# A fused attention block on one core: weights' sums, one load's place and the order of the tokens' small steps in setup and batches 0 and 1

## The chip, the cores and the metric

The kernel runs on one core of one Trainium2 chip. The metric is the device time of one execution, in microseconds (us); lower is better. Time before: 973.11 us, the median of 3 runs (971.55 to 974.76).

## What is computed

For each of 16 batches there are 100 rows `x` of 640 numbers and a context of 722 rows of 384. The last 4 context rows are "tokens" (`ca`), the other 718 are `enc`. All arithmetic is float32. Cut to what matters:

```
hs     = mha(x @ Wq, enc @ Wk, enc @ Wv)              # 8 heads of 80, 718 keys
ca_q1  = einsum("btc,th->bch", ca, Wq_ca)[:, picked]  # 100 picked columns of the tokens
ca_hs1 = mha(ca_q1, x, x)                             # first token attention
hs2    = mha(ca_hs1 @ Wq, ca @ Wk_ca, ca @ Wv_ca)     # second token attention, 4 keys
out    = (hs + hs2) @ Wout + b_out + x
mha    = softmax(q k^T / sqrt(80)) v, head by head
```

## The kernel before

**Products with fewer multiplications.** The context of a batch, seen as 3 thirds of the rows by 3 chunks of 128 columns, is multiplied with Wk and with Wv, each seen as 3 chunks by 2 halves. A bilinear scheme does this with 15 products in place of 18. Each product takes a form of the context (7 are raw pieces, the others are sums of pieces, made by `enc_sums`, L466 to L485, 13 operations on GpSimd) and a form of the weights (6 raw, others made by `weight_sums`, L487 to L506: 7 "early" ones that fill unused slots and 5 "late" ones, some of which overwrite raw pieces). `V_PLAN` (L93) and `K_PLAN` (L111) give the order of the products, the PSUM bank of each (A to E), and where the bank's content is moved to afterwards. The first move to a place is a copy on ScalarE (L392), a later one an addition on VectorE (L390). `Keys.go(n)` and `Values.go(n)` issue the next n products with their moves. A bank that was opened goes on collecting, so its next product must come after the move of the content before it.

**Batch 0 is different.** Its values (`first_values`, L353) and its keys (`first_keys`, L561) are made plainly from raw pieces, because the sums don't exist yet. Two of its six value blocks (0 and 3) are made only inside batch 0, between the key products of batch 1.

**Setup (L256 to L1082).** Loads go out on SP, in an order that is partly fixed. TensorE makes `first_values`, a matrix `m` for the tokens (L1007), the tokens' products `y_ps` (L721), and turns the packed Wk by transposes into `w_ps` (L1030). Five copies of `w_ps` into `wk_sb` and `wk4` go alternately to ScalarE and VectorE (L1033). On VectorE stand also 15 copies that rearrange Wq (L1041, L1048). Then come the first keys, `va_ps`, and the queries of batches 0 and 1.

**The loop over batches (L1090).** One batch, in the order of TensorE: scores `s_ps` (L598, three groups, each moved to SBUF by ScalarE), the first token attention's `z_ps` (L783), the next batch's token products `y_ps` (L721), the transposes of the batch before, then the products of this batch's values and the next batch's keys in turn, `last_keys` (L568), the output projection of the batch before, on odd batches the next queries (L519), and last `a_ps` (L1267), the probabilities times the values.

- `Maximum` (L634) makes the maximum over the keys, for each head and query, in five steps (`top.go`), mostly on VectorE. `subtract(i)` and `exponential(i)` turn the scores into probabilities on VectorE and ScalarE; `larger(i)` keeps the running maximum.
- The tokens' small steps belong to the class `Second` (L703): `scores1` (7 operations of GpSimd, L756 and L763), `softmax1` (VectorE, 8 steps of a `Maximum` and a subtraction), `exponentials1` (ScalarE), `softmax2` (L778), `scores2` (3 operations of VectorE and an exponential of ScalarE), `softmax3` (3 of VectorE) and `values2` (7 of GpSimd, L845 and L852). `load` brings the token values `vb` by GpSimd's DMA queue (L802; one buffer).
- `keys(m)` (L691, 5 operations of GpSimd) prepares a batch's token keys. `loads()` (L1096) asks for the batch after next: `ca`, the context (`load_enc`, L213: three transfers, two buffers) and `mb` (`load_m`, L682, two buffers). `load_rest` (L223) asks for the two pieces of the context that have a buffer of their own, `rest`, of which there is one. An mb load waits until `keys` has read the buffer's content.

**What sets the order.** From L1089 on, TensorE, VectorE, ScalarE and GpSimd issue in the order of the Python text (`manual_schedule`). Before that line, and on SP throughout, a planner chooses the order from its own estimate of when things are ready. `tc.issue_after(ins)` keeps what its block holds behind `ins` on that engine, and `wait_for(a, b)` (L623) makes `a` wait for `b`.

Of the kernel before, what the change touches and what calls it, by code (L numbers as in the profile page):

```python
# [14 lines left out]
B, S, H = 16, 100, 640  # L15
# [7 lines left out]
KT = SK // 3 + 1  # L23
# [101 lines left out]
def kernel(  # L125
# [63 lines left out]
    def hsT_tile(name):  # L189
        return main.tile([P, HC, P], F32, tag="hsT", name=name, bufs=2)  # L190
# [19 lines left out]
    def rest_tile(name):  # L210
        return main.tile([P, len(A_REST), KT], F32, tag="rest", name=name)
# [9 lines left out]
        return enc  # L221

    def load_rest(b, enc):  # L223
        rest = rest_tile(f"rest_{b}")
        for (u, c), i in A_REST.items():
            nc.sync.dma_start(
                out=rest[:, i], in_=enct[b][:, c, u * (KT - 1) : u * (KT - 1) + KT]
            )
        return enc[0], rest
# [257 lines left out]
    def weight_sums(engine, w, late):  # L487

        at = lambda f: w[:, W_AT[f]]
        raw = lambda c, g: w[:, 2 * (c - 1) + g - 1]  # L490
        for out, left, right in (
            (at(5), raw(2, 2), raw(1, 2)),
            (at(14), raw(2, 1), raw(2, 2)),
            (at(7), raw(3, 2), at(5)),
            (at(3), raw(1, 1), at(7)),
            (at(13), raw(3, 1), at(7)),
        ) if late else (
            (at(0), raw(1, 2), raw(1, 1)),
            (at(1), raw(2, 1), raw(3, 1)),
            (at(2), raw(1, 1), raw(2, 2)),  # L500
            (at(6), raw(2, 1), raw(1, 1)),
            (at(10), raw(3, 1), raw(2, 2)),
            (at(11), raw(2, 2), raw(3, 2)),
            (at(12), raw(3, 2), raw(3, 1)),
        ):
            engine.tensor_tensor(out, left, right, ALU.subtract)  # L506
# [54 lines left out]
    def first_keys(enc):  # L561
        for n in range(HC - 1):
            banks = [psum(f"kT_ps_0_{n}_{k}") for k in range(2)]
            weights = [wk_sb[:, 2 * c + n % 2, n // 2] for c in range(CC)]
            chunk_keys(n, banks, weights, enc)
        last_keys(0, enc)
# [460 lines left out]
    for c in range(HC):  # L1027
        w_ps = psum(f"w_ps_{c}")
        for cc in range(CC):
            nc.tensor.transpose(  # L1030
                w_ps[:, cc * P : (cc + 1) * P], wkt_sb[:, c, cc * P : (cc + 1) * P], ident
            )
        (dve if c % 2 else act)(  # L1033
            wk_sb[:, c % 2 : 6 : 2, c // 2] if c < HC - 1 else wk4,
            w_ps[:, : CC * P].rearrange("p (a n) -> p a n", a=CC),
        )

    with tc.issue_after(summed.ins):
        for c in range(HC):
            for u in range(2):  # L1040
                nc.vector.tensor_copy(  # L1041
                    wq_sb[:, c, 2 * u * P : 2 * (u + 1) * P].rearrange(
                        "p (a r k) -> p a r k", a=2, r=RG
                    ),
                    wq_in[c].rearrange("p (r k) -> p r k", r=RG)[:, :, u * D : u * D + 64]
                    .rearrange("p r (a k) -> p a r k", a=2),
                )
            nc.vector.tensor_copy(  # L1048
                wq_sb[:, c, 4 * P :].rearrange("p (h k) -> p h k", h=NH),
                wq_in[c].rearrange("p (h k) -> p h k", h=NH)[:, :, 64:],  # L1050
            )
    first_keys(enc)

    va = wide("va")[:, : H // 2]
    va_ps = psum("va_ps")
# [34 lines left out]
    for b in range(B):  # L1090
# [38 lines left out]
        if b == 0:  # L1129
            now.load()  # L1130
            now.softmax1()
            for late in (False, True):
                weight_sums(nc.vector, wk_sb, late)
            enc_sums(enc)
            weight_sums(nc.gpsimd, wv_sb, False)
        st.append(scores(b, 0, tiles))
        if b == 0:
            now.exponentials1()
# [14 lines left out]
            kk = Keys(b + 1, enc)  # L1153

        if b == 0:
            now.scores2()
            now.softmax3()
            second.scores1()
            top.go(3)
            kk.go(3)  # L1160
            top.go(1)
            first_values(3, e_in, (act, act), (0,), bank)
            kk.go(2)
            top.go()
            first_values(3, e_in, (act, act), (1,), bank)
            kk.go(3)
            first_values(0, e_in, (act, act), (0,), bank)
            kk.go(2)
            subtract(0)
            exponential(0)  # L1170
            first_values(0, e_in, (act, act), (1,), bank)
            kk.go(2)
            subtract(1)
            kk.go(3)
            exponential(1)
            second_next, enc_next, m_next = loads()
            last_keys(b + 1, enc)
            subtract(2)
            exponential(2)
            now.values2()  # L1180
            second.load()
            second.softmax1(4)
        elif b + 1 < B:
            last.transpose()
            vv = Values(b, e_in)

            def both(n):
                vv.go(n)
                kk.go(n)

            second.scores1(seen)
            last.load()
            top.go(3)
            both(3)
            now.scores2()
            top.go(1)
            both(2)
            top.go()
            both(2)
            both(1)  # L1200
            now.softmax3()
            now.values2()
            vv.go(2)
            kk.go(1)
            subtract(0)
            exponential(0)
            both(2)
            vv.go(1)
            kk.go(2)
            both(1)  # L1210
            both(1)
            second.load()
            second_next, enc_next, m_next = loads()
            subtract(1)
            exponential(1)
            last_keys(b + 1, enc)
            subtract(2)
            exponential(2)
            second.softmax1()
            last.project()  # L1220
        else:
            room = enc_tile("spare").rearrange("p f k -> p (f k)")
            spare.extend(room[:, i * H : (i + 1) * H] for i in range(2))
            last.transpose()
            vv = Values(b, e_in)
            last.load()
            mine.load()
            top.go(3)
            vv.go(3)
            now.scores2()  # L1230
            top.go(1)
            vv.go(2)
            top.go()
            vv.go(3)
            now.softmax3()
            now.values2()
            vv.go(2)
            subtract(0)
            exponential(0)
            vv.go(5)  # L1240
            for i in (1, 2):
                subtract(i)
                exponential(i)
            last.project()
        if b + 2 < B:
            enc_next = load_rest(b + 2, enc_next)
            keys(m_next)
            enc_sums(enc_next)
# [97 lines left out]
```

## Time and profile before

| What | Value |
|---|---|
| median of the runs, with lowest and highest | 973.11 us (971.55 to 974.76) |
| the profiled execution's own time | 972.35 us |
| its span, from the first to the last instruction | 970.6 us |
| TensorE clock granted, mean | 0.993 of full speed |
| TensorE matmul busy | 942.7 us |
| VectorE, GpSimd, ScalarE busy | 674.4, 627.4, 359.5 us |
| moved by DMA | 62.48 MB in 45255 packets |

The profile is of one execution. Its engines are PE (TensorE matmuls), PEld (TensorE weight loads), DVE (VectorE), ACT (ScalarE), POOL (GpSimd) and SP (SyncE, which only issues transfers here). A "q" behind an engine's name is its sequencer, as in SPq for a transfer that SP issues. In a line of a timeline stand the start and the length in us, the engine, the line of the code, the operation, what it writes and reads, and in brackets how long the engine had been idle and who ended that. Times count from the start of the span. An adjacent run of equal instructions is shown as one line with its count. The lines that matter are shown in the prediction.

### The profile page before, as it was taken

The page shows a single profiled execution, that of the slowest core. Times are in us where ns is not written, and L with a number is a line of the kernel's source. Part 1 is how long each engine was busy: PE and PEld are TensorE (multiplying, and loading weights), DVE is VectorE, ACT ScalarE, POOL GpSimd, SP SyncE. Part 2 cuts the span into 40 slices and gives each one's busy share as a digit, 9 for nine tenths or more (in the row PEclk, how much of TensorE's full clock was granted, in tenths as well). Part 3 has the DMA queues.
Part 4 walks back from the last instruction along what each step waited for, and adds up shares of the span by engine and source line. Part 5 has one row for each costly group of instructions (what it writes and reads, how often), then busy time and mean ns, then how long its engine had stood idle before and what let it go on. Part 6 is the DMA issues. An engine that isn't in the chain of part 4 may idle for free.

```text
span 970.6 us, 25628 instructions
## 1 busy us (share of the span) xinstructions
PE 942.7 (97%) x11215; PEld 803.1 (83%) x11215; DVE 674.4 (69%) x1083; ACT 359.5 (37%) x596; POOL 627.4 (65%) x572
## 2 busy tenths in 40 slices
PE   8898879999999999999999999999999999999998
PEld 5797868988788888978889887897879888897866
DVE  1358769586856868587874868668784877838783
ACT  1134424433334343342534334343432534324341
POOL 4269877594963758487673958638694576737522
PEclk9999999999999999999999999999999999999999
DMA  7840213113030211213031030301103030300101
GB/s 244 286 146 23 66 34 92 32 25 103 8 119 24 71 58 28 73 29 120 9 105 38 8 121 8 119 24 49 52 29 99 8 102 17 85 27 1 58 1 35
DMA packets 45255, 62.48 MB, mean 64 GB/s; under 512 B 13336, under 2 KB 37208, under 8 KB 43544
## 3 DMA queue, kind: packets, MB, share of 16 engines
q1 hardware_dynamic: 41608, 42.97, 14.9%
q0 software_dynamic: 2512, 16.72, 5.5%
q8 instruction: 88, 1.44, 0.6%
q10 hardware_dynamic: 1024, 1.15, 0.4%
q14 instruction: 23, 0.19, 0.1%
HBM read 55.26 MB, written 5.57 MB: 63 GB/s over the span
## 4 chain that ended last, share of the span: by engine, by line
PE 81%; POOL 7%; DMA 4%; DVE 3%; SPq 2%; ACT 1%; issue 1%; ACTq 0%; DVEq 0%; POOLq 0%
PE a_ps L1267 11%; PE s_ps L598 10%; PE v_psA L419 9%; PE v_psB L419 8%; PE k_psA L450 7%; PE o_ps L926 7%; PE q_ps L519 6%; PE k_psB L450 6%; PE kT_ps L543 5%; PE v_psC L419 3%; PE k_psC L450 2%; POOL enc L485 2%; PE v_psE L419 1%; POOL e L756 1%; PE y_ps L721 1%; PE v_psD L419 1%
## 5 line engine op out<-in xcount | busy, mean ns | idle before, releaser
L756 POOL TENSOR_TENSOR e<-ca,g 100x800 f32<-100x800 f32 x64 | 99.4, 1563 | 147.5 <-DVE most L1124 131.9
L845 POOL TENSOR_TENSOR hs<-vb,p 100x640 f32<-100x640 f32 x64 | 105.6, 1660 | 43.9 <-DVE p L831 41.3
L1267 PEld LDWEIGHTS a_ps<-vs,st 120*64 120x64 f32 (+3 forms) x3072 | 112.4, 127 | 11.1 <-ACT st L1120 5.9
L1267 PE MATMUL a_ps<-vs,st 120*64 120x81 f32 (+3 forms) x3072 | 115.6, 237 | 5.4 <-ACT st L1120 5.4
L419 PE MATMUL v_psA<-wv_sb,enc 128*120 128x320 f32 x360 | 112.1, 434 | 1.5 <-DVE vs L390 1.5
L1112 DVE TENSOR_TENSOR st<-st,over 120x1600 f32<-120x1600 f32 x48 | 106.2, 2236 | 0.0
L485 POOL TENSOR_TENSOR enc<-enc 128x240 f32<-128x240 f32 x135 | 98.6, 745 | 7.1
L485 POOL TENSOR_TENSOR enc<-enc,rest 128x240 f32<-128x240 f32 x45 | 40.0, 888 | 95.6 <-DMA rest<-in_enct 82.0
L598 PE MATMUL s_ps<-qp,kT 32*120 32x100 f32 x3072 | 97.4, 263 | 0.0
L598 PEld LDWEIGHTS s_ps<-qp,kT 32*120 32x120 f32 x3072 | 94.7, 179 | 1.6 <-issue 0.2
L763 POOL TENSOR_TENSOR e<-e,e 100x800 f32<-100x800 f32 x48 | 93.3, 1943 | 3.8
L450 PE MATMUL k_psA<-enc,wk_sb 128*128 128x240 f32 x360 | 88.8, 370 | 6.2 <-POOL enc L485 3.4
L419 PE MATMUL v_psB<-wv_sb,enc 128*120 128x320 f32 x300 | 93.1, 433 | 0.0
L615 ACT COPY st<-s_ps 120x800 f32<-120x800 f32 x64 | 49.7, 829 | 114.8 <-PE s_ps L598 114.8
L450 PEld LDWEIGHTS k_psA<-enc,wk_sb 128*128 128x128 f32 x360 | 68.6, 191 | 24.0 <-POOL enc L485 3.9
L419 PEld LDWEIGHTS v_psA<-wv_sb,enc 128*120 128x120 f32 x360 | 64.5, 183 | 24.7 <-DVE vs L390 2.7
L1124 DVE TENSOR_TENSOR most<-most,st 120x800 f32<-120x800 f32 x64 | 65.5, 1023 | 23.0 <-ACT st L609 21.9
L1120 ACT ACTIVATE st<-st 120x1600 f32<-120x1600 f32 x48 | 74.0, 1542 | 17.9 <-DVE st L1112 17.9
L852 POOL TENSOR_TENSOR hs<-hs,hs 100x640 f32<-100x640 f32 x48 | 77.1, 1607 | 3.8
L450 PE MATMUL k_psB<-enc,wk_sb 128*128 128x240 f32 x300 | 73.9, 369 | 0.0
L1278 DVE RECIPROCAL rs<-a_ps 100x4 f32<-100x4 f32 x32 | 5.8, 182 | 97.7 <-PE a_ps L1267 97.6
L419 PEld LDWEIGHTS v_psB<-wv_sb,enc 128*120 128x120 f32 x300 | 54.8, 183 | 22.3 <-DVE vs L390 0.5
(138 smaller groups left out, 1791.5 us busy)
## 6 DMA issues: line engine op xcount, KB each, us to landing
vb<-va_d POOLq DMA_DIRECT2D x16, 1000.0 KB, 5.9
enc<-in_enct SPq DMA_DIRECT2D x30, 240.0 KB, 3.8
enc<-in_enct SPq DMA_DIRECT2D x15, 360.0 KB, 3.7
xT<-in_xt SPq DMA_DIRECT2D x8, 500.0 KB, 3.5
rest<-in_enct SPq DMA_DIRECT2D x31, 120.0 KB, 3.6
xn<-in_x SPq DMA_DIRECT2D x11, 320.0 KB
out<-xn SPq DMA_DIRECT2D x11, 320.0 KB, 2.5
ca<-in_cas SPq DMA_DIRECT2D x16, 156.2 KB
```

Of the source, the lines that this page charges most:

```text
L419: nc.tensor.matmul(at[0][j][:KN, : H // 2], a_form(self.enc, f)[:, j * KN : (j + 1) * KN], wv_sb[:, W_AT[f]], start=first, stop=last, skip ...
L450: nc.tensor.matmul(at[:, i * KT : (i + 1) * KT], wk_sb[:, W_AT[f], i], a_form(self.enc, f), start=(first and i == 0), stop=last, skip_grou ...
L485: nc.gpsimd.tensor_tensor(out, left, right, op)
L598: nc.tensor.matmul(s_ps[r][:n, 256 * a + lo : 256 * a + hi], kT[rows, c, u, j * KN : (j + 1) * KN], rhs, start=(a == 0 and c == 0), stop=( ...
L756: first = nc.gpsimd.tensor_tensor(to, self.ca[:, t, :].unsqueeze(1).to_broadcast([S, NH, S]), g[:, :, t].unsqueeze(2).to_broadcast([S, NH, ...
L763: nc.gpsimd.tensor_tensor(e, e, to, ALU.add)
L845: first = nc.gpsimd.tensor_tensor(to, vb[:S, t, :].rearrange("p (h d) -> p h d", h=NH), p2[:, :, t].unsqueeze(2).to_broadcast([S, NH, D]), ...
L852: nc.gpsimd.tensor_tensor(sums, sums, to, ALU.add)
L926: nc.tensor.matmul(o_ps[:n, k, : H // 2], hsTs[r][:, c, :n], wout_sb[:, c, k * (H // 2) : (k + 1) * (H // 2)], start=(c == 0), stop=(c == ...
L1112: return nc.vector.tensor_tensor(st[i], st[i], top.over[:KN].unsqueeze(1).to_broadcast([KN, 2, ROWS]), ALU.subtract,)
L1120: nc.scalar.activation(st[i], st[i], AF.Exp, scale=SCALE)
L1267: nc.tensor.matmul(a_v[lo:hi, h % 4], st[i // 2][: KEYS[i], i % 2, h * S + lo : h * S + hi], block(i, h // 4)[: KEYS[i], h % 4], start=(i ...
```

## The change

It has five parts, all in setup and in batches 0 and 1:

1. All five copies of `w_ps` go to ScalarE.
2. The early sums of Wk and Wv go to VectorE in setup, behind the first token product's reduction (`summed`) and ahead of `first_keys` in the text; the late ones of Wk follow `first_keys`. They stood at the head of batch 0, those of Wk on VectorE and the early ones of Wv on GpSimd. The late sums of Wv stay in batch 1.
3. `rest_1` gets a buffer of the tag `hsT`, which at that time holds a part of `m`, so that `rest` is free for `rest_2`.
4. In batch 0, batch 1's `scores1` and `kk.go(3)` come ahead of `top.go(3)`, then `scores2`; `softmax3` comes five steps later.
5. At the end of batch 0, `load_rest(2)` and `keys` come ahead of `values2`, which now waits for `subtract(2)`; `enc_sums` for batch 2 stands right behind it. The load of `vb_1` moves from batch 0 into batch 1, behind `scores1` there.

```diff
     def load_rest(b, enc):
-        rest = rest_tile(f"rest_{b}")
+        if b == 1:
+            room = hsT_tile("rest_1").rearrange("p c s -> p (c s)")
+            rest = room[:, : len(A_REST) * KT].rearrange("p (i k) -> p i k", k=KT)
+        else:
+            rest = rest_tile(f"rest_{b}")
...
-        (dve if c % 2 else act)(
+        act(
             wk_sb[:, c % 2 : 6 : 2, c // 2] if c < HC - 1 else wk4,
...
+    for w in wk_sb, wv_sb:
+        with tc.issue_after(summed.ins):
+            weight_sums(nc.vector, w, False)
     first_keys(enc)
+    weight_sums(nc.vector, wk_sb, True)
...
         if b == 0:
             now.load()
             now.softmax1()
-            for late in (False, True):
-                weight_sums(nc.vector, wk_sb, late)
             enc_sums(enc)
-            weight_sums(nc.gpsimd, wv_sb, False)
...
         if b == 0:
+            second.scores1()
+            kk.go(3)
+            top.go(3)
             now.scores2()
-            now.softmax3()
-            second.scores1()
-            top.go(3)
-            kk.go(3)
             top.go(1)
             first_values(3, e_in, (act, act), (0,), bank)
             kk.go(2)
             top.go()
             first_values(3, e_in, (act, act), (1,), bank)
             kk.go(3)
+            now.softmax3()
             first_values(0, e_in, (act, act), (0,), bank)
...
             last_keys(b + 1, enc)
-            subtract(2)
+            less = subtract(2)
             exponential(2)
-            now.values2()
-            second.load()
+            enc_next = load_rest(b + 2, enc_next)
+            keys(m_next)
+            now.values2(less)
+            enc_sums(enc_next)
             second.softmax1(4)
...
             second.scores1(seen)
+            if b == 1:
+                now.load()
             last.load()
...
-        if b + 2 < B:
+        if 0 < b < B - 2:
             enc_next = load_rest(b + 2, enc_next)
             keys(m_next)
             enc_sums(enc_next)
```

## The prediction

> **What bounds the kernel now.** I read the page first, for which engine fills the span; then TensorE's waits in the first 165 us; then the timelines of TensorE, SP, GpSimd, VectorE and ScalarE around each wait; last the granted clock in short windows.
>
> ```profile
> span 970.6 us, 25628 instructions
> ...
> PE 942.7 (97%) x11215; PEld 803.1 (83%) x11215; DVE 674.4 (69%) x1083; ACT 359.5 (37%) x596; POOL 627.4 (65%) x572
> ```
>
> ```profile
> PE k_psA L450 <- POOL enc L485: 3.4, 1, 3.4
> PE z_ps L783 <- issue: 3.2, 1, 3.2
> ...
> PE a_ps L1267 <- ACT st L1120: 1.8, 1, 1.8
> ...
> PE k_psA L450 <- ACT kT L392: 1.5, 1, 1.5
> PE k_psA L450 <- DVE kT L390: 1.3, 1, 1.3
> ...
> PE kT_ps L543 <- DVE wk_sb L1033: 1.0, 1, 1.0
> ```
>
> TensorE is busy for 97% of the span, so only what shortens its gaps or its slow stretches counts. Its waits (engine and line, who ended the wait, us in total, times, longest) are few, and nearly all lie before 135 us. From 136 to 190 us it is busy for 54.00 of 54.00 us. The last waits, near 907 and 933 us, are not touched.
>
> How the 3.4 us wait arises is read from SP, GpSimd and TensorE in order of time (start us, duration us):
>
> ```profile
> 118.05 0.38 SPq L686 DMA_DIRECT2D mb<-m_d  x1
> 118.52 3.61 SPq L217 DMA_DIRECT2D enc<-in_enct  x3
> 122.22 0.89 SPq L226 DMA_DIRECT2D rest<-in_enct  x2
> ...
> 126.09 1.40 POOL L485 TENSOR_TENSOR enc<-enc,rest 128x240 f32<-128x240 f32 x1 [8.07 <-DMA rest<-in_enct]
> ...
> 123.20 0.39 PE L783 MATMUL z_ps<-y,e 100*32 100x33 f32 x23 [3.18 <-issue]
> ...
> 131.81 1.97 PE L450 MATMUL k_psA<-enc,wk_sb 128*128 128x240 f32 x4 [3.41 <-POOL enc L485]
> 133.57 1.81 PE L450 MATMUL k_psB<-enc,wk_sb 128*128 128x240 f32 x4
> ```
>
> SP's queue holds batch 2's context load (L217) behind an mb load (L686) that waits for `keys(m_next)`. GpSimd reaches that only after `values2` (104.2 to 114.9). So the data land at 126, the sums start then, and batch 1's first key product starts at 131.8. The gap of 3.18 us inside z_ps is charged to no engine; it falls while the 1000 KB vb load (issued at 114.88) and the enc load keep the DMA engines over 90% busy.
>
> Clock, in stretches laid so that the half-clock ones are met whole (stretch, length, PE busy, PEld, DVE, ACT, POOL, granted clock, DMA):
>
> ```profile
> 32.60:36.00 3.40, 1.36 (x9) 0.95 (x9) 0.93 (x4) 0.96 (x2) 0.00 (x0) 1.00 1.03 361
> 36.00:39.40 3.40, 3.31 (x9) 2.82 (x10) 2.87 (x15) 0.00 (x0) 0.00 (x0) 0.54 0.88 323
> ...
> 101.10:104.50 3.40, 1.57 (x27) 1.09 (x27) 1.63 (x2) 2.36 (x3) 3.40 (x2) 1.00 0.20 47
> 104.50:107.90 3.40, 3.40 (x58) 3.40 (x55) 3.23 (x9) 0.00 (x0) 3.32 (x3) 0.51 0.00 0
> ...
> 121.50:124.90 3.40, 1.70 (x37) 1.66 (x38) 2.35 (x7) 0.00 (x0) 0.00 (x0) 1.00 0.78 218
> ```
>
> Each stretch that TensorE fills to 1.57 us or less is followed by one at half clock; after 1.70 us it is not.
>
> [...] the first enc sum takes 3.78 us beside the weight sums of L506, against some 0.7 us later.
>
> **The change, part by part**
>
> *First keys.* The kT_ps group at 36.09 waits for VectorE's copy of w_ps chunk 1, which stands behind a wq_sb copy that waits for its DMA (35.07); the group needs that bank. On ScalarE, idle in 1.30 and 0.76 us pieces there, the copy (0.48 us) is done near 33.1. TensorE starts at about 35.1, after the last transpose: **-0.95**. That also lifts the window 32.6 to 36.0 from 1.36 to about 2.3 us busy, above the 1.70 that stayed warm. Then the four products from 36.09 to 39.30 take 4 x 0.405 = 1.62 us (the pace after 39.3) instead of 3.2: **-1.6**. If the clock still drops, that is 0.
>
> *Weight sums on VectorE.* Added before and after the first keys: 7 for wk and 7 for wv early, 5 for wk late. At 0.416 us (wk row) and 0.483 (wv row), less about 0.08 of overlap, that is 7 x 0.34 + 7 x 0.42 + 5 x 0.34 = 7.0 us. VectorE is idle from 38.9 to 57.3. The early 14 end near 44.5, before GpSimd starts at 45.1. The late 5 need the first keys' fourth chunk read (about 50) and lie beside GpSimd's `scores1`, whose additions grow from 1.88 to 3.3 us under such company: it ends some 1.6 us later, at 59. The softmax chain behind it (8.3 us before, 1.2 of it a wait for a buffer) then ends near 66; ScalarE wants it at about 68.3, after the score copies. Price nothing, with 2 us of cover; past it 1 us each. Removed: 5.6 us of VectorE at 65.65 to 71.25, 5.8 us of GpSimd at 82, and the stretching of the enc sums.
>
> *rest_1 in another place.* Its two issues (0.85 us) leave their place ahead of enc_1 on SP if SP takes them earlier, and rest_2 no longer waits for batch 1's sums. SP's ca load stands ahead of enc_1 and waits for `scores1` (55.36, later about 57): enc_1 would issue at 59.5 to 60 and land near 66 (before: 58.80 and 65.4). The seventh sum, which the first key product needs, then ends near 72 (7 x 0.75 plus some contention); TensorE comes at 73.1. Price 0, at most 1, and the wait of two rows below would absorb that.
>
> *Order in batch 0.* With `kk.go(3)` ahead of `scores2`, ScalarE copies the first key bank at once instead of behind an exponential that waits for VectorE: the 1.5 us wait goes. Next late is VectorE: after `larger(2)` (76.4 with the 2.55 us from above and 0.3 less contention) come 3.4 us of `top.go(3)`, 1.4 of `scores2`, 0.66 of the addition, so the third A product starts near 81.9 instead of 86.17. Of that 4.2 us, 2.55 was counted above: **-1.65**. The 1.3 us wait stays, and `softmax3` moves behind the additions, where VectorE has room. The 1.8 us wait of a_ps stays too: ScalarE's two kT copies (0.82) and the exponential (1.54) follow the last key product whatever VectorE does. Its half clock costs 8.04 - 6.97 x 176/192 = 1.65 us; the window lies about as before, I count 0, with -1.65 for the low end.
>
> *Loads, and batch 1.* GpSimd loses the 5.8 us of wv sums and does `scores1` (16.5), `keys` (2.55), then `values2`, which now waits for `subtract(2)`, and behind it the sums of enc_2 and all of batch 1's `scores1`. Scores1 ends near 93, keys near 95.5; SP then issues enc_2 at 96, landing at 103.6 (7.6 us as before). `subtract(2)` ends at 102.5 - 4.2 = 98.3, `values2` at 109 (10.7), the seventh sum at 115.3 (6.3, as from 126.09). TensorE wants it at 128.4 - 4.2 - 3.2 = 121. With 5.7 us to spare, the 3.41 us gap goes and, with it, the half clock (4.22 us for three pairs of products against 2.43): **-5.2**. The vb_1 load moves behind batch 1's `scores1` (about 133)[...], and enc_2's load falls on keys and a_ps; in later batches enc loads beside a_ps show no issue gap. So the z_ps gap goes: **-3.2**. vb_1 lands near 139, `values2` of batch 1 starts then instead of at 148. Without the gaps, VectorE's five wv sums (2.2 us) ahead of z and g in batch 1 delay v_psD's bank: **+0.4** (0 to 0.8).
>
> Sum: -0.95 - 1.6 - 1.65 - 5.2 - 3.2 + 0.4 = **-12.2 us**. The profiled execution took 972.35 (span 970.6 and 1.75 around it): 960.15. The median shown, 973.11, is 0.76 above it: **960.9**.
>
> **The rivals**
>
> *A, the fetch gap stays (0.15).* [...] Against: one in 16 batches. 3.2 us back: 964.1.
>
> *B, the enc sums are still late (0.10).* SP's order is not written out, and enc_2 may stand behind something slower. For: it did before. Against: 5.7 us of cover. Gap and half clock back: 966.1.
>
> *C, the clock pays differently (0.13).* The setup drop stays (962.5), or the one in a_ps goes too (959.2).
>
> *D, slower (0.04).* `values2` waits for `subtract(2)` and holds GpSimd's whole queue. If VectorE's order delays `subtract(2)`, each us after the first 5.7 holds TensorE a us. It must come 5.7 + 12.2 + 3 = 21 us late for a loss: at 119 instead of 98, giving 976. Nothing in VectorE's queue there is that long (its longest, L1112, is 3.5 us).
>
> *E, nothing (0.03).* What hid behind the removed gaps fills them: within 2.9 us of 973.
>
> **How the numbers follow.** Likeliest 960.9 (0.55). A measurement of this kernel tells about 0.3%, 2.9 us, from no change. A, B and C end faster as well: faster 0.93, same 0.03, slower 0.04. The range runs from 958.0 (the likeliest less 1.65, and the other small terms) to 966.0, at B's edge; past it and below it lie some 2 in 10.
>
> **What would show it.** No wait at the first kT_ps, and full clock from 35 to 39 us; no wait for ScalarE's kT copy, one of about 1.3 us for VectorE's; no GpSimd wait for rest, enc_2 issued near 96; no issue gap in z_ps; k_psA of batch 1 at 0.97 us a group. I am wrong if enc_1 lands past 67, if SP's order holds enc_2, or if a new half-clock stretch appears before 140 us.

## The result, and the profile after

The changed kernel takes **962.92 us** (median of 4 runs, 962.5 to 965.66); the kernel before took 973.25 us beside it (4 runs, 971.55 to 974.76). The ratio is 0.99 with a 95% interval of 0.9876 to 0.9925: about 10.3 us, or 1%, faster. The prediction said 960.9 us, 2.0 us less than measured.

The profiled execution of the changed kernel took 962.5 us, its span is 960.8 us, and the mean granted clock is 0.995. The head of its page:

```profile
span 960.8 us, 25628 instructions
...
PE 940.9 (98%) x11215; PEld 801.5 (83%) x11215; DVE 682.6 (71%) x1088; ACT 360.1 (37%) x598; POOL 620.8 (65%) x565
```

TensorE is busy 1.8 us less than before. That is about one stretch at half clock, which costs 1.7 us by my estimate (3.41 us at a granted clock of 0.50): in the profiled execution three such stretches of the kernel before (at 36.28, 104.54 and 131.85 us) are gone and two new ones (at 23.25 and 118.83) have come. The other 8 us of the span are waits that are gone. The waits of TensorE in the first 160 us of the changed kernel (engine and line, who ended the wait, us in total, times, longest):

```profile
PE v_psA L423 <- DVE wv_sb L510: 2.9, 1, 2.9
...
PE a_ps L1276 <- ACT st L1128: 1.6, 1, 1.6
...
PE k_psA L454 <- POOL enc L489: 0.7, 1, 0.7
PE k_psA L454 <- DVE kT L394: 0.5, 1, 0.5
```

The issue gap in `z_ps`, the wait for ScalarE's kT copy and the one at the first kT_ps are no longer in the list. GpSimd's enc sums still hold a `k_psA`, but for 0.7 us and in batch 0; VectorE's kT wait fell from 1.3 to 0.5. At the top stands a wait that the kernel before did not have: the first value product of batch 1 waits 2.9 us for a late sum of Wv.

The end of batch 0 and the head of batch 1 in the timelines of SP, GpSimd, VectorE and TensorE (start us, duration us):

```profile
96.50 0.38 SPq L690 DMA_DIRECT2D mb<-m_d  x1
96.97 1.75 SPq L217 DMA_DIRECT2D enc<-in_enct  x3
...
98.24 2.50 POOL L849 TENSOR_TENSOR hs<-vb,p 100x640 f32<-100x640 f32 x2 [1.76 <-DVE st L1120]
108.90 0.69 POOL L489 TENSOR_TENSOR enc<-enc,rest 128x240 f32<-128x240 f32 x1
112.96 3.48 POOL L489 TENSOR_TENSOR enc<-enc 128x240 f32<-128x240 f32 x3
...
113.00 2.90 DVE L1132 TENSOR_TENSOR most<-most,st 120x800 f32<-120x800 f32 x2 [1.31 <-ACT st L613]
115.82 4.57 DVE L510 TENSOR_TENSOR wv_sb<-wv_sb 128x320 f32<-128x320 f32 x5
...
113.50 0.75 PE L787 MATMUL z_ps<-y,e 100*32 100x33 f32 x64
114.18 1.21 PE L725 MATMUL y_ps<-m,xT 128*100 128x96 f32 x10
115.22 0.59 PE L902 MATMUL hst_ps<-ident,hs 100*128 100x100 f32 x5
118.74 2.38 PE L423 MATMUL v_psA<-wv_sb,enc 128*120 128x320 f32 x4 [2.93 <-DVE wv_sb L510]
120.91 1.90 PE L423 MATMUL v_psB<-wv_sb,enc 128*120 128x320 f32 x4
122.65 1.24 PE L423 MATMUL v_psD<-wv_sb,enc 128*120 128x320 f32 x4
123.73 0.97 PE L454 MATMUL k_psA<-enc,wk_sb 128*128 128x240 f32 x4
```

The upper part went as the prediction worked it out: context load near 96 (96.97), `values2` 98.3 to 109 (98.24 to 108.9), the seventh enc sum near 115.3 (116.44), in time for the key product. The lower part did not. `z_ps` runs without a gap and TensorE reaches `v_psA` at about 115.8, but VectorE starts the five late Wv sums only at 115.82, and they take 4.57 us. In the kernel before the same five took 2.21 us, under cover of the issue gap:

```profile
118.97 2.02 DVE L1124 TENSOR_TENSOR most<-most,st 120x800 f32<-120x800 f32 x2 [1.40 <-ACT st L609]
120.90 2.21 DVE L506 TENSOR_TENSOR wv_sb<-wv_sb 128x320 f32<-128x320 f32 x5
```

TensorE waits for the third, and the two groups of products behind it are slow (2.38 and 1.90 us where the kernel before took 1.26 and 1.24).

The granted clock shows it too (stretch, length, PE busy, PEld, DVE, ACT, POOL, clock, DMA share, GB/s; changed kernel):

```profile
32.60:36.00 3.40, 2.69 (x19) 2.20 (x20) 0.72 (x4) 2.39 (x6) 0.94 (x4) 1.00 0.99 356
36.00:39.40 3.40, 3.40 (x18) 3.20 (x17) 2.70 (x15) 0.79 (x3) 0.00 (x0) 1.00 0.83 317
...
97.70:101.10 3.40, 1.76 (x50) 1.60 (x47) 3.26 (x8) 2.13 (x3) 2.78 (x3) 1.00 0.92 259
101.10:104.50 3.40, 3.40 (x103) 3.40 (x100) 3.29 (x8) 0.00 (x0) 3.24 (x3) 1.00 0.06 20
...
114.70:118.10 3.40, 1.11 (x13) 0.92 (x11) 3.40 (x4) 0.51 (x1) 3.32 (x4) 1.00 0.00 0
118.10:121.50 3.40, 2.76 (x6) 1.69 (x7) 3.33 (x7) 0.33 (x2) 3.24 (x5) 0.61 0.00 0
```

The first pair is the setup: 2.69 us busy, then full clock. The second pair is `a_ps`: after 1.76 us busy the half clock that followed there before (0.51) is gone. The third pair is new: 1.11 us busy, then 0.61.

A second new stretch lies earlier in setup, where TensorE makes `m`. These two lines are laid on the change of the clock itself:

```profile
19.84:23.25 3.41, 0.80 (x24) 0.69 (x20) 1.21 (x5) 0.00 (x0) 0.00 (x0) 1.00 0.59 226
23.25:26.66 3.41, 3.41 (x14) 3.41 (x15) 0.35 (x1) 0.00 (x0) 0.00 (x0) 0.50 0.61 189
```

It makes the first `y_ps` late (31.43 instead of 29.70). Little of that reaches the first keys, because the last transposes wait for a Wk transfer all the same, until 35.03 (34.58 before).

Laid side by side by the starts of TensorE's groups, the two spans differ as follows (before to after, us):

| Stretch of TensorE | before | after | difference |
|---|---|---|---|
| start to first kT_ps | 36.09 | 35.39 | -0.70 |
| first kT_ps to `va_ps` (first keys) | 20.11 | 18.32 | -1.79 |
| `va_ps` to the third `k_psA` of batch 0 | 29.97 | 28.32 | -1.65 |
| from there to `a_ps` of batch 0 | 15.44 | 15.44 | 0 |
| `a_ps` to `s_ps` of batch 1 | 10.58 | 8.75 | -1.83 |
| `z_ps` to `y_ps` | 4.05 | 0.68 | -3.37 |
| `y_ps` to `v_psA` | 1.47 | 4.56 | +3.09 |
| `v_psA` to `k_psA` | 6.82 | 4.99 | -1.83 |
| three pairs of key products | 4.22 | 2.43 | -1.79 |
| all the rest | | | +0.07 |
| span | 970.6 | 960.8 | -9.8 |

### The profile page after: what moved, and what is told of

Read it like the earlier page. It is cut to its first block, busy times and chain, and to the rows that moved or that the text cites. A ratio compares the mean times of both kernels' runs of the same rounds, so it can differ in the third digit from the quotient of the medians.

```text
span 960.8 us, 25628 instructions
## 1 busy us (share of the span) xinstructions
PE 940.9 (98%) x11215; PEld 801.5 (83%) x11215; DVE 682.6 (71%) x1088; ACT 360.1 (37%) x598; POOL 620.8 (65%) x565
## 4 chain that ended last, share of the span: by engine, by line
PE 91%; DVE 4%; DMA 2%; SPq 2%; ACT 1%; issue 0%; ACTq 0%; DVEq 0%
PE a_ps L1276 12%; PE s_ps L602 11%; PE v_psA L423 10%; PE v_psB L423 8%; PE k_psA L454 7%; PE kT_ps L547 7%; PE q_ps L523 7%; PE o_ps L930 7%; PE k_psB L454 6%; PE v_psC L423 3%; PE k_psC L454 3%; PE v_psE L423 2%; PE v_psD L423 2%; PE y_ps L725 2%; DMA kT<-in_wkt 1%; PE k_psE L454 1%
## 5 line engine op out<-in xcount | busy, mean ns | idle before, releaser
L489 POOL TENSOR_TENSOR enc<-enc 128x240 f32<-128x240 f32 x135 | 103.6, 781 | 7.1
L489 POOL TENSOR_TENSOR enc<-enc,rest 128x240 f32<-128x240 f32 x45 | 37.0, 822 | 87.1 <-DMA rest<-in_enct 78.7
L767 POOL TENSOR_TENSOR e<-e,e 100x800 f32<-100x800 f32 x48 | 90.5, 1885 | 3.8
L454 PEld LDWEIGHTS k_psA<-enc,wk_sb 128*128 128x128 f32 x360 | 68.2, 190 | 18.3 <-DVE kT L394 1.0
L1132 DVE TENSOR_TENSOR most<-most,st 120x800 f32<-120x800 f32 x64 | 66.6, 1040 | 23.3 <-ACT st L613 22.2
```

The costliest lines, as they stand in the source:

```text
L454: nc.tensor.matmul(at[:, i * KT : (i + 1) * KT], wk_sb[:, W_AT[f], i], a_form(self.enc, f), start=(first and i == 0), stop=last, skip_grou ...
L489: nc.gpsimd.tensor_tensor(out, left, right, op)
L767: nc.gpsimd.tensor_tensor(e, e, to, ALU.add)
```

## The experiments

The theory after this comparison: the prediction's terms hold, and the time missing is the late Wv sums, which stand where TensorE needs them at once. Its rival: VectorE is full in this stretch, so that sums put elsewhere only move the wait. Beside these, the runs test what the single parts bring, and three smaller theories: that the wait in front of `values2` pays by keeping GpSimd away from VectorE (P), that issue gaps come with transfers that fill the DMA engines (F; their share in the gap of the kernel before is 0.90), and that the half clock follows from how little TensorE was filled (C). Times are medians; ratios are against the kernel before in the same series, with 95% intervals.

### The late sums elsewhere

**Sums in batch 0, behind `subtract(2)`:**

```diff
             less = subtract(2)
+            weight_sums(nc.vector, wv_sb, True)
...
-        if b == 1:
-            weight_sums(nc.vector, wv_sb, True)
```

> The changed kernel with the late sums of Wv moved from batch 1 into batch 0, right behind subtract(2) on VectorE. Theory T (in the changed kernel batch 1's first value product waits for these sums themselves, which run at half speed beside GpSimd's enc sums): the wait of 2.9 us at v_psA goes, and with it the half-clock stretch behind it (1.8 us), so 4.7 us less than the changed kernel: about 958.2 us against 973.2 for the kernel before. Rival R (VectorE's queue is late at that place whatever stands in it, and only the name of the wait changes): the wait stays within 1 us of 2.9, under another name, and the time stays at 962 to 963.

Measured: 964.7 us, ratio 0.9908 (0.9892 to 0.9924), no better than the whole change. The profiled execution took 960.66 us, the other four 963.51 to 965.63. From the waits, then the timelines of VectorE and TensorE in this run:

```profile
PE s_ps L602 <- DVE hs L1288: 2.5, 1, 2.5
```

```profile
97.11 6.68 DVE L510 TENSOR_TENSOR wv_sb<-wv_sb 128x320 f32<-128x320 f32 x5
...
112.50 0.94 PE L602 MATMUL s_ps<-qp,kT 32*120 32x100 f32 x25 [2.48 <-DVE hs L1288]
```

The wait at `v_psA` and its reduced clock are gone: from `z_ps` to the key product TensorE takes 5.40 us instead of 10.23, as expected. But the five sums took 6.68 us beside `values2`, and all that VectorE had behind them came later, in the end the products that free `a_ps`'s banks; the scores waited. From `a_ps` to `z_ps` it is 19.46 us instead of 16.03. So this stretch keeps 1.4 of the 4.8 us, and an issue gap of 1.1 us in batch 0 takes most of that. The other four executions took 2.9 to 5.0 us longer than this one. Their mean granted clock is 0.992 to 0.995, against 0.999 in the profiled one; where the clock fell in them is not on record.

**Sums ahead of the maximum in batch 1:**

```diff
+        if b == 1:
+            weight_sums(nc.vector, wv_sb, True)
         larger(1)
...
-        if b == 1:
-            weight_sums(nc.vector, wv_sb, True)
```

> The changed kernel with the late sums of Wv still in batch 1, but ahead of larger(1) on VectorE in place of behind it. T says the first value product finds its weights by 116 and does not wait; z and g come as late as before (120 to 121), so the wait moves to v_psD, whose banks hold z_ps and y_ps: 2.5 to 3.5 us there, time about as the changed kernel, 962 to 963.5. R says the wait at v_psA stays.

Measured: 961.4 us, ratio 0.9883 (0.987 to 0.9896), a little below what was expected. The waits of this run:

```profile
PE v_psD L423 <- DVE z L798: 1.6, 1, 1.6
...
PE k_psE L454 <- DVE vs L394: 1.0, 1, 1.0
```

The sums start at 113.24 and `v_psA` doesn't wait; `z`, `g` and the later moves of banks do come later, and the wait turns up at `v_psD` (1.6 us) and `k_psE` (1.0 us). From `z_ps` to the key product it is 7.25 us, between the 10.23 of the change and the 5.40 without any wait.

**Sums behind `a_ps`'s products, at the very end of batch 0:**

```diff
         if b == 0:
+            weight_sums(nc.vector, wv_sb, True)
             nc.vector.tensor_tensor(hs[:S], hs[:S], hs2, ALU.add)
```

(with the block of batch 1 removed as above)

> The changed kernel with the late sums of Wv at the end of batch 0 on VectorE, behind the reciprocals and products of a_ps and ahead of the addition of hs2, where VectorE idled for 1.9 us in the changed kernel. Theory T (the sums themselves hold batch 1's first value product, and placed behind subtract(2) they held the end of a_ps instead): no wait at v_psA, none of over 1 us at s_ps, no half-clock stretch there; 4.0 to 4.7 us less than the changed kernel, about 958.5. Rival (VectorE has no room anywhere between batch 0 and 1, the lost time only moves): a wait of 2 us or more at z's or y's bank (v_psD) or at s_ps, time 961 to 963.

Measured: 960.86 us, ratio 0.9876 (0.986 to 0.9891). VectorE and TensorE in this run:

```profile
107.08 4.52 DVE L510 TENSOR_TENSOR wv_sb<-wv_sb 128x320 f32<-128x320 f32 x5
...
115.86 1.26 PE L423 MATMUL v_psA<-wv_sb,enc 128*120 128x320 f32 x4
...
119.11 0.97 PE L454 MATMUL k_psA<-enc,wk_sb 128*128 128x240 f32 x4
...
129.74 1.08 PE L454 MATMUL k_psE<-enc,wk_sb 128*128 128x240 f32 x4 [0.98 <-DVE vs L394]
```

Neither `s_ps` nor `v_psA` waits and the clock stays full: the key product starts at 119.11, 4.6 us earlier than in the change. By the next queries 3.3 us of that are left (149.39 against 152.64), because `k_psE` waits for VectorE's moves; an issue gap of 1.1 us in batch 0's `z_ps` takes more. The median is 2.1 us lower, half of what was expected (the profiled execution took 959.87). The interval overlaps that of the change, which was timed in another series; what shows the gain is the trace, not the medians alone.

**And `scores2` of batch 1 later:** the run before with

```diff
-            now.scores2()
+            if b > 1:
+                now.scores2()
             top.go(1)
             both(2)
+            if b == 1:
+                now.scores2()
```

> The kernel of e9 with, in batch 1 only, scores2 behind the second pair of value and key products in place of ahead of it. Theory: in e9 VectorE has become the bound of batch 1 (k_psE waits 0.98 us for its additions, which stand behind scores2, 1.5 to 2.2 us); with scores2 later that wait goes and nothing replaces it, 1.0 to 1.4 us less than e9: 959.6. Rival (the additions are held by top.go itself, or ScalarE's spread comes late instead): a wait of about 1 us stays at k_psE or moves to a later product, time as e9, 960.5 to 961.

Measured: 959.57 us, ratio 0.9861 (0.9843 to 0.9879), as expected, and the lowest median of all. The interval overlaps that of the run before, so here too it is the trace that shows the step. The wait at `k_psE` fell from 0.98 to 0.3 us, and from `z_ps` to the next queries it is 34.52 us (35.78 in the run before, 39.14 in the change); a `z_ps` issue gap of 1.7 us in batch 0 remains. So the wait behind the late sums was VectorE's own queue: three steps less ahead of the moves, and it shrinks. Behind the gap in batch 0 comes a stretch at half clock (columns as above):

```profile
69.47:72.88 3.41, 1.75 (x92) 1.35 (x86) 2.35 (x2) 1.69 (x3) 3.33 (x4) 1.00 0.00 0
72.88:76.29 3.41, 3.41 (x14) 3.16 (x15) 2.01 (x4) 0.37 (x1) 3.25 (x5) 0.50 0.13 16
```

### The parts one by one

**The `vb_1` load alone**, in the kernel before:

```diff
             now.values2()
-            second.load()
...
             second.scores1(seen)
+            if b == 1:
+                now.load()
```

> The kernel before with one thing changed: the load of vb_1 in batch 1, behind scores1 there. Theory F [...]: the issue gap goes or falls under 1 us. But the enc sums still set the start of the first key product, so the wait there grows from 3.4 to about 6, and the time falls by at most 0.6 us (one DMA issue of GpSimd that no longer stands ahead of keys): 972.6 to 973.2. Rival (the two gaps add): 3.2 us less, 970.0. If the gap has another cause it stays at 3.2.

Measured: 974.05 us, ratio 1.0014 (1.0004 to 1.0023), no gain: if anything a little slower than the kernel before. The profiled execution took 971.13, the least of 14. From its waits, then TensorE's timeline:

```profile
PE k_psA L450 <- POOL enc L485: 7.5, 2, 6.9
```

```profile
103.37 6.41 PE L1268 MATMUL a_ps<-vs,st 119*64 119x81 f32 x176 [1.64 <-ACT st L1120]
...
120.76 1.31 PE L419 MATMUL v_psA<-wv_sb,enc 128*120 128x320 f32 x4 [0.40 <-DVE wv_sb L506]
```

The gap in `z_ps` went as foreseen, and the wait at batch 1's first key product grew from 3.41 to 6.94 us: TensorE only arrived earlier at a place where it had to wait anyway. The prediction's -3.2 for the gap was a gain only together with the -5.2 behind it. Two more things can be read here. With GpSimd idle beside them, the late sums hold `v_psA` for only 0.40 us, although no gap covers them. And `a_ps` runs at full clock (6.41 us, 8.04 in the kernel before), although the load that moved comes after it.

**The order in batch 0 alone** (part 4 of the change, in the kernel before):

```diff
+            second.scores1()
+            kk.go(3)
+            top.go(3)
             now.scores2()
-            now.softmax3()
-            second.scores1()
-            top.go(3)
-            kk.go(3)
```

(and `softmax3` five steps later)

> The kernel before with the new order of scores2, kk.go(3) and softmax3 in batch 0 alone. The wait of 1.5 us for ScalarE's kT copy goes, the wait of about 1.3 us for VectorE's stays, and a_ps starts some 1.6 us earlier. Theory G (GpSimd's queue, not TensorE, sets the start of batch 1's first key product in the kernel before): all of it is given back there, that wait grows from 3.4 to about 5, time 973.2 as before, within 0.4. Rival (the gaps add): 1.6 us less, 971.6.

Measured: 970.32 us, ratio 0.9976 (0.9963 to 0.999), where about nothing was expected. The waits are those expected (ScalarE's kT wait gone, VectorE's 2.1 us, 4.8 us for the enc sums). But SP's queue had changed:

```profile
104.44 1.74 SPq L217 DMA_DIRECT2D enc<-in_enct  x3
121.64 0.37 SPq L686 DMA_DIRECT2D mb<-m_d  x1
122.11 1.87 SPq L226 DMA_DIRECT2D rest<-in_enct  x2
```

The planner now put the context load ahead of mb, 14 us earlier than before; only `rest` still came late. No issue gap appeared, and `a_ps` ran at full clock (6.41 us). The -2.3 us can't be told apart into these and the reordering; it isn't the price of part 4 by itself.

**Loads and the end of batch 0 alone** (parts 3 and 5) and **setup alone** (parts 1 and 2), each in the kernel before, with the hunks of the diff shown in the section on the change:

> The kernel before with only the other place for rest_1, and the end of batch 0 changed (load_rest and keys ahead of values2, which waits for subtract(2), enc_sums right behind, vb_1 later). Theory G: the enc sums now end near 124 in place of 132, so the 3.4 us wait goes and so does the issue gap of 3.2 us in z_ps, but the late sums of Wv then hold v_psA by about 2 us. In all 4 to 7.6 us less: 967.6 as the middle. Rival (setup's and batch 0's edits are needed for any gain, as GpSimd still does the early sums of Wv): within 1.5 us of before.

> The kernel before with only the copies of w_ps on ScalarE and the weights' sums in setup. Theory S: first keys start 0.7 to 1 us earlier and run at full clock (1.6 us); GpSimd, without 5.8 us of wv sums and the stretching of the enc sums, reaches keys some 10 us earlier (about 107), so enc_2 lands near 115 and the 3.4 us wait and its half clock (5.2) go too, while the late sums of Wv hold v_psA as in the changed kernel (up to 4.7 back). Sum 3 to 8 us less, 966 as the middle; this would show that setup's part alone brings half or more of the change. Rival (setup brings its own 2.5 us and no more, the loads wait as before): 970.

Measured: 969.1 us, ratio 0.9959 (0.9943 to 0.9975), and 967.06 us, ratio 0.9935 (0.992 to 0.995), each 1 to 1.5 us short of the middle of what was expected. The profiled executions took 971.37 and 968.54, the most of six in both. From the waits of the first, then of the second:

```profile
PE v_psA L423 <- DVE wv_sb L510: 2.5, 1, 2.5
```

```profile
PE v_psA L419 <- DVE wv_sb L506: 2.1, 1, 2.1
...
PE s_ps L598 <- issue: 1.4, 1, 1.4
```

Each of them alone takes the enc wait away, one by an earlier load, the other by taking 5.8 us of Wv sums off GpSimd, and in each the wait at `v_psA` for the late sums appears. From `z_ps` to the end of the three pairs of key products the kernel before takes 16.56 us, the first 12.50, the second 12.54, the change 12.66. So both bring the same 4 us there, which can be had once: the parts alone come to -3.8, -5.8 and -2.3, together -11.9, where the whole brings -10.3. The difference of 1.6 us is less than the 4 us they share; what makes up for the rest is not shown.

### The smaller theories

**Without the wait of `values2`**, in the version with the sums behind `a_ps`:

```diff
-            now.values2(less)
+            now.values2()
```

> The kernel of e9 with values2 in batch 0 not waiting for subtract(2). Theory P (GpSimd and VectorE stretch each other): values2 starts 1.7 us earlier and lies beside subtract(2), which grows from 1.9 to about 3.4 us; the exponential behind it and with it a_ps come 1 to 1.5 us later (and the clock may halve there, 1.6 more), while the enc sums come 1.7 us earlier, which nothing needs: 1 to 3 us more than e9, 962 to 964. Rival (the two don't meet on the path; last_keys' copies on ScalarE set the exponential): within 0.5 us of e9.

Measured: 960.16 us, ratio 0.9869 (0.9852 to 0.9886), against 960.86 with the wait, which the intervals do not tell apart. GpSimd and VectorE in this run:

```profile
96.21 4.08 POOL L849 TENSOR_TENSOR hs<-vb,p 100x640 f32<-100x640 f32 x2
...
96.03 1.89 DVE L1120 TENSOR_TENSOR st<-st,over 120x1600 f32<-120x1600 f32 x1
```

Side by side, VectorE's subtraction takes 1.89 us as ever, and GpSimd's two operations are the ones stretched, from 2.50 to 4.08 us. Whether it waits 1.76 us or is slowed by 1.58, GpSimd ends at about the same time: P fell, the wait neither costs nor brings anything that can be measured.

**The `vb_1` load back in batch 0**, in the same version:

```diff
             now.values2(less)
+            second.load()
             enc_sums(enc_next)
...
-            if b == 1:
-                now.load()
```

> The kernel of e9 with the load of vb_1 back in batch 0, behind values2 and ahead of the enc sums. Theory F (the issue gap of the kernel before came from vb's and enc's transfers together[...]): enc_2 has landed by 104 and vb alone is in flight from 108 to 115, so the gap in z_ps or s_ps is under 1.5 us or absent; GpSimd's issue takes 0.6 us: 0 to 1.5 us more than e9. Rival (vb's load alone causes the gap): 3 us in z_ps or s_ps, 964.

Measured: 960.2 us, ratio 0.9866 (0.9846 to 0.9885). From TensorE's timeline in this run:

```profile
117.01 0.39 PE L787 MATMUL z_ps<-y,e 100*32 100x33 f32 x24 [0.83 <-issue]
```

With the load back at its place a gap is back before the last 24 products of `z_ps` (23 in the kernel before), at 0.83 us instead of 3.18. Behind the issue of the vb load (109.38) the DMA share is 0.74 from 110 to 114 us, and 0.06 from 114 to 118, where the gap lies: the transfers had all but ended when it came. So in this run full DMA engines beside the gap are not what makes it, and F needs a link between the two. In the kernel before, one record near the gap could be such a link: a packet of the queue that the profile calls instruction (q8) starts early in it. This line is the DMA view from 120.5 to 120.6 us (packets, MB, share of the 16 engines):

```profile
q8 instruction: 1, 0.02, 72.9%
```

It takes 1.2 us, and the gap ends 1.5 us behind it. The q8 packet ahead of it had started 7.4 us earlier, and in the 4 us ahead of the packet the DMA share was 0.89. But in the traces of the kernel before and of the change 14 q8 packets (from 10 us on) had a DMA share of 0.8 or more in the 4 us ahead of them, and only this one has an issue gap of 0.8 us or more around or behind it. That TensorE waited for this packet is my estimate; it was not shown. The gap of 0.83 us doesn't show in the time.

**Copies of `w_ps` in turn again**, the change without its part 1:

```diff
-        act(
+        (dve if c % 2 else act)(
```

> The changed kernel with the copies of w_ps again in turn on ScalarE and VectorE. Theory: the first kT_ps group waits 0.7 to 1 us for VectorE, the window before it is then less than half busy and the first four products run at half clock (1.6 us): 1 to 2.6 us more than the changed kernel, 964 to 965.5. Rival (the last wkt transfer sets the start of the first keys anyway, and the clock drops or not by chance): within 0.5 us of the changed kernel.

Measured: 966.71 us, ratio 0.9932 (0.9916 to 0.9948): 3.8 us more than the change, where 1 to 2.6 were expected. The wait for VectorE at the first kT_ps is back (0.6 us), and half clock with it (0.50 from 36 to 40 us, 1.00 in the change). Of the difference, 2.0 us lie between the first kT_ps and `va_ps` (20.33 us instead of 18.32). The first kT_ps starts 1.75 us later, and there a Wk transfer has its part: the transposes waited 2.4 us for it in this execution, 0.3 in that of the change.

**The same with useless work:** 14 products of a 128x128 tile with itself, into a bank nobody reads, between and behind the transposes.

```diff
+    def filler(n):
+        with tc.issue_after(turned.ins):
+            for _ in range(n):
+                nc.tensor.matmul(fill[:, :P], idle, idle, start=True, stop=True)
...
+        if c > 1:
+            filler(6 if c == 2 else 2)
...
+    filler(4)
```

> The kernel of e8 (the changed kernel with the copies of w_ps in turn on both engines) with 14 filler products of 128 by 128 among and behind the transposes of w_ps: 6, 2, 2 and 4, written to a bank that nothing reads. They add work and no data. Theory C (what the kernel before and e8 lose at the first keys is mostly the half clock behind a stretch that is under half busy): with the fillers TensorE stays at full clock from 34 to 41 us, the first keys take 18.3 us from their first product to va_ps in place of 20.1 to 20.3, and the time falls to 963 to 965 against 966.7 for e8, although the copies alternate. Rival (the half clock has another cause, or the wait for VectorE's copy is the loss): the stretch stays at half clock or the time stays at 966 to 967, or rises by the fillers' 3 us.

Measured: 963.05 us, ratio 0.9899 (0.9881 to 0.9916), 3.7 us less than without the filler. Stretches of 2 us (columns as above), without the filler and with it:

```profile
34.00:36.00 2.00, 1.72 (x8) 1.53 (x9) 0.00 (x0) 0.38 (x1) 0.00 (x0) 0.55 1.02 391
36.00:38.00 2.00, 1.38 (x5) 0.92 (x4) 1.88 (x7) 0.58 (x2) 0.00 (x0) 0.50 1.00 385
38.00:40.00 2.00, 2.00 (x6) 1.66 (x6) 1.93 (x12) 0.00 (x0) 0.00 (x0) 0.50 0.82 308
```

```profile
34.00:36.00 2.00, 1.87 (x16) 1.51 (x14) 0.98 (x4) 0.48 (x1) 0.00 (x0) 1.00 1.02 382
36.00:38.00 2.00, 1.96 (x10) 1.85 (x11) 1.83 (x10) 0.00 (x0) 0.00 (x0) 1.00 0.76 289
```

TensorE does more and is done sooner: the clock is 1.00 instead of 0.50 to 0.55, the first kT_ps starts at 36.04 instead of 37.14, and from there to `va_ps` it is 18.42 instead of 20.33 us. These 1.9 us are the clock. The earlier start is only in part: the Wk transfer that the transposes waited for also landed earlier here (they begin at 32.74 instead of 34.28). But the mean granted clock is 0.996 to 0.998 in all four executions with the filler and 0.992 or 0.993 in all four without. So C is shown, for these first keys, by adding work that carries no data.

## Why the prediction was right, and where it was not

The direction and most of the terms were as predicted; the sum was 2.4 us too good (-12.2 against -9.8 between the profiled executions), and one term holds the fault. One of its own signs of being wrong came, a new half-clock stretch before 140 us: at 118.8, behind the late sums (and one at 23.3, in setup).

- **First keys, -0.95 and -1.6.** Measured -0.70 and -1.79. The last Wk transfer came 0.45 us later in this execution, so its start alone is no clean test, but all the traces together are. With all copies on ScalarE the first kT_ps starts between 34.1 and 35.6 us (eight executions), with copies in turn between 36.0 and 38.1 (six). From there to `va_ps` it is 20.1 us or more in all five with copies in turn and no filler, and 18.3 in six of the eight with copies on ScalarE. In the other two (sums ahead of the maximum, and setup alone) half clock came all the same, and it is 19.9 and 19.2. So both terms are real, and the second is likely rather than certain.
- **Weight sums in setup, priced at nothing.** They hid. (In the sum, 0.483 less 0.08 is 0.40 and not 0.42; nothing hangs on it.) What went the other way: GpSimd's additions beside the five late Wk sums stayed at 1.88 to 1.94 us instead of growing to 3.3, while VectorE's sums took up to 1.98 us each instead of 0.34. `scores1` ended at 57.6, 1.4 us earlier than priced.
- **rest_1 elsewhere, 0 to 1, and order in batch 0, -1.65.** The context load went out at 59.00, the enc wait came out at 0.67 us, and the VectorE wait shrank from 1.26 to 0.47 to absorb it: -1.65 for the stretch, as worked out.
- **Enc wait and half clock at batch 1's key product, -5.2, and the issue gap, -3.2.** Both went. The seven enc sums took 7.5 us instead of 6.3 (in the kernel before they had taken 5.7, from 126.09 to 131.76), and the cover of 5.7 us was enough for that. The gap gave -3.37. The other is hidden in the table by the new stall: `v_psA` to `k_psA` would be 3.41 us shorter, and the three pairs are 1.79 shorter.
- **Half clock in `a_ps`, counted 0, -1.65 for the low end.** It went: -1.83. This was luck, not something that the prediction derived: in the run with the vb load alone, which changes nothing ahead of `a_ps`, it went as well (6.41 us, where the same code took 8.04 in the profiled execution of the kernel before).
- **The step that failed: "VectorE's five wv sums (2.2 us) ahead of z and g in batch 1 delay v_psD's bank: +0.4 (0 to 0.8)".** Measured +4.67: 3.09 us from `y_ps` to `v_psA`, and 1.58 us between `v_psA` and `k_psA` (4.99 us, where the kernel before takes 3.41 without its wait), for the reduced clock that followed. Two things were missed. First, *who reads*: the first value product of batch 1 itself takes a weight form that the third late sum makes; the prediction looked at the bank that stands behind `z`, not at the operand. Second, *how long*: 2.2 us was measured while GpSimd stood idle, waiting for `rest`. The change moved GpSimd's enc sums to just this place, and the five took 4.57 us; the two steps of the maximum ahead of them took 2.9 us instead of 2.0. By my estimate, at the pace of the kernel before the third sum would have ended near 116.2 instead of 118.6, and TensorE, there at 115.8, would have waited some 0.5 us. So some 2.4 of the 2.9 us are VectorE slowed down, and some 0.5 are the place. The run with the vb load alone bears this out: there GpSimd was idle, and the wait was 0.40 us. In the five runs with the late sums at this place and enc sums beside them it was 2.1 to 2.9. The prediction had read such a stretching from the kernel before (3.78 us for the first enc sum beside weight sums on VectorE, some 0.7 us later), allowed for it in setup, and didn't apply it here.

The errors of +4.3 here and -1.83 at `a_ps` nearly make up the 2.4 us. The runs with the sums elsewhere show that the stall is the sums, since it goes when they move. They also show that the rival was half right: VectorE is nearly full there, and of the 4.7 us nothing (behind `subtract(2)`), 1.5 (sums ahead of the maximum), 2.1 (behind `a_ps`) and 3.4 (with `scores2` later as well) came out in the medians.

Of the rivals in the prediction, A (the issue gap stays) and B (late enc sums) did not come. C came in its second form, with the drop in `a_ps` gone. D's condition, a late `subtract(2)`, was not met: it ended at 98.2 (98.3 worked out). The gap went when the load was moved: it is 3.18 us in the kernel before, and there is none in the run with the vb load alone. What TensorE waited for in it no trace shows: the prediction's name for it, "fetch gap", is an estimate, and 13 other packets of the instruction queue behind DMA engines about as full brought no gap.

## What to carry to other kernels

When a stall is removed, walk through each queue that used to run under its cover and ask which operand, not only which buffer, the first instruction behind it reads. A duration measured while the neighbour engine stood idle isn't the duration once the change puts work there (2.21 us for the five sums, then 4.57): take it from a row with the same company. And gains of two stalls in a row on the same path belong together: the first removed alone (3.2 us of gap) brought nothing.

## What the runs showed of the hardware that was not expected

- **Useless products can pay.** 14 of them in setup brought 3.7 us (963.05 against 966.71), of which the trace shows 1.9 as the clock.
- **Half clock came in stretches of 3.41 us.** In the clock records of the kernel before, stretches at 0.50 start at 36.28, 104.54, 131.85 and 910.09 us, in those of the change at 23.25, 118.83 and 900.48. Each lasts 3.41 us, and they start 20, 8 and 228, then 28 and 229 times 3.41 us apart. In the 3.41 us right ahead of these seven TensorE was busy 1.56, 1.59, 0.04, 1.47, 0.80, 0.48 and 1.49 us. In the same two traces, cut into stretches of 3.41 us in step with these, the clock stayed full behind each with 1.77 us or more, and behind one with 1.43 (19.21 to 22.63 in setup of the kernel before). In the run with `scores2` later half clock came after 1.75 us (lines there). In the run with copies in turn and no filler it lasted longer (0.55, 0.50 and 0.50 in the three stretches of 2 us from 34 to 40). So the border at 1.57 to 1.70 that the prediction read off is not sharp. The 3.18 us gap in the kernel before lay across two of these stretches, with 1.82 and 1.83 us busy, and the clock stayed at 1.00.
- **Which of VectorE and GpSimd is stretched varies.** VectorE's 128x320 sums took 0.44 us each alone and 0.91 beside enc sums; a 128x256 sum took up to 1.98 (0.42 alone) beside `scores1`, which was hardly slowed (1.94 us for an addition, 1.88 in the kernel before); beside `subtract(2)` GpSimd was slowed (2.50 to 4.08 us for two) and VectorE wasn't (1.89). In the last two cases the one that started second was the slow one: the sum of 1.98 us started 0.24 us behind an addition of `scores1` and ended 0.28 us behind it; GpSimd's first product started 0.18 us behind `subtract(2)`.
- **Issue gaps wander.** 3.2 us in `z_ps` of batch 1 before; 1.4 us in `s_ps` with setup alone changed; 1.1 to 1.7 us in `z_ps` of batch 0 in four of the runs with moved sums. Loads ran ahead of them where the DMA share was read: 1.04 from 110 to 114 us ahead of the one in `s_ps` (it ends at 116.6), 0.64 and 0.73 from 66 to 70 us ahead of two of those in batch 0 (they end at 72.2 and 72.3). The change had 0.79 from 66 to 70 us and no gap.
- **An edit elsewhere reorders SP.** With only the order of batch 0 changed, a context load went out 14 us earlier. This is the planner's doing, not the chip's.
- **Setup varies by itself.** With the same setup code, the first kT_ps started between 34.1 and 35.6 us over seven profiled executions, half clock came among the first keys in one of them (2.61 us for the first six products, 1.38 in the others) and in `m_ps` in two (8.49 us, 6.84 to 6.87 in the others). That is as large as some of the differences discussed here.
